# Conv and dynamic-filter layers over four images: norm statistics of all images in the first conv stage, six product buffers, every second broadcast by transfer

## The chip, the cores and the metric

The kernel runs on one core of one Trainium2 chip. The metric is the device time of one execution in microseconds (us); the median of three runs is the time of a kernel. The profile is of one further execution.

## The reference

Two layers over x of 4 images, 256 channels, 48 x 48, all in float32 (shortened):

```python
# layer 0
g = group_norm(x, 32 groups)                  # over 8 channels and all pixels
h = relu(batch_norm(conv3x3(g, conv_w) + conv_b))
q, k, v = einsum(qkv_w, h) + qkv_b            # 8 heads of 32
attn = softmax(q^T k * 32**-0.5)              # 2304 x 2304 per head
x = x + proj_w @ (v attn^T) + proj_b
# layer 1
g = group_norm(x, 32 groups)
guidance = conv3x3(g, W_cat)                  # 45 maps: 9 for each dilation
outs = [g]
for i, d in enumerate((1, 6, 12, 24, 36)):
    w = softmax(guidance[:, 9*i:9*i+9], axis=1)
    outs.append(sum over the 9 taps k of shifted(g, d, k) * w[:, k])
y = conv1x1(concat(outs), W_scale)            # 1536 -> 256 channels
x = x + batch_norm_over_all_images(y)
```

## The kernel before, in words

Channels lie on the 128 partitions in two halves (NH = 2); the 48 rows of an image go in six chunks of eight rows (NCK = 6, CH = 384 pixels). The order of instructions on each engine is written out by the program (a manual schedule): what is emitted first on an engine runs first, and waits are put in where data need them.

The main loop runs over b = 0 to 4. In step b the program emits, in one stretch, the filters of image b-1 (layer 1) merged with the conv and q, k, v of image b (layer 0), and after it the attention of image b. So the stages in time are: the conv stage of image 0 alone; attention 0; joint stretch 1 (filters of image 0, conv of image 1); attention 1; joint stretch 2; attention 2; joint stretch 3; attention 3; the last stretch (filters of image 3 alone); and the end, where y of all images is scaled and added.

**The conv stage** (`conv_qkv`, `conv`) makes a 3 x 3 convolution with transformed rows: TensorE's matmuls (line 851) go through two PSUM banks (tag "c"), ScalarE and VectorE take the results (lines 797 to 820), `relu` writes `hid`, then q, k (line 884) and v (line 905) are made. In the conv stage of image 0 VectorE also makes the transformed weights, which SP stores to memory (line 716) and later stretches read back (line 679); from image 1 on GpSimd instead of VectorE forms the transformed inputs.

**The first norms.** The conv of an image needs the group norm of its x. For image 0 it is made at the very start. For the others `stats_of` loads the image in twelve pieces of 128 x 384 through two buffers (`xst`, line 1519, on SP's queue) and takes `bn_stats` of each (line 605, VectorE). `first_norms` is a generator that makes them one step at a time; `merged` puts one step between matmuls whenever the conv's matmul time has grown by a given amount (from 40 000 ns on, each 2000 ns in the first conv stage, each 4000 ns later). In step 0 it makes images 1 and 2, in step 1 image 3. `Norm.finish` turns the sums of one image into mean and reciprocal deviation: `bn_aggr` (VectorE), a matmul with the group matrix, a copy and two squares (ScalarE), two more matmuls, then add, square root (ScalarE, with its table) and reciprocal. Image 1 is finished in step 0; images 2 and 3 are finished in the prologue of joint stretches 1 and 2, at the places called `beside` in `dynamic_filters`.

**The filters** (`dynamic_filters`). The softmaxed filter maps of a chunk are in a tile `w`, and are stored to memory too (`w_d`). Each chunk has 36 to 39 taps, 222 in a stretch. For each tap:

1. the filter map is broadcast to all partitions in a PSUM bank `wb` (three banks in joint stretches): by a TensorE matmul with a one-hot column (line 1406); or, for a third of the taps (list `sent`), by a transfer that reads `w_d` into a buffer `wbs` (three buffers, issued on ScalarE's queue, line 1351) and a ScalarE copy into PSUM (line 1403);
2. VectorE multiplies it with the shifted input (`prod`, line 1463), through five buffers (PRODS); the first tap of each dilation goes straight to `cat` (line 1437);
3. GpSimd adds the product to `cat` (line 1480). A "split" tap is divided: VectorE does one half whole (lines 1447, 1449), GpSimd adds the other (line 1452).

Finished `cat` tiles go through the 1 x 1 convolution (`mix`, line 1290), whose result is copied to y (line 1317).

**The planner.** While it emits, the program keeps a clock for PE, DVE, ACT and POOL (`Clock`), with a cost for each instruction, and decides by it: `fill` lets TensorE do conv work of the next image until the next `wb` bank is free; a tap is split when GpSimd would end over 4500 ns (SPLIT) after VectorE; and a sent broadcast goes through ScalarE only where it would be in time:

```python
late = max(clock.t["ACT"], spot + 150, there + 150) + 300
if (c, k) in number and late <= max(clock.t["DVE"], clock.t["PE"], spot + 150):
```

Here `there` is the issue plus 3000 ns and `spot` the time at which the bank is free. Otherwise the matmul is emitted, though the transfer was made. `fetch` issues transfers up to three sent broadcasts ahead, as far as the buffers reach and the chunk's filters are made.

Of the kernel before, what the change touches and what calls it, by code (L numbers as in the profile page):

```python
# [8 lines left out]
F32 = mybir.dt.float32  # L9
F32R = mybir.dt.float32r  # L10
AF = mybir.ActivationFunctionType
# [4 lines left out]
B, C, HH, WW = 4, 256, 48, 48  # L16
N = HH * WW
P = 128
NH = C // P
# [4 lines left out]
CH = R * WW  # L24
NCK = N // CH
# [9 lines left out]
SAFE = 60.0  # L35
LENT = (2, 5, 8, 11, 14)
CATS = 4
PRODS = 5
SLACK = 3000.0
SPLIT = 4500.0  # L40
BEHIND = 0.0
# [7 lines left out]
def conv_preact_kernel(  # L49
# [12 lines left out]
    nc = tc.nc  # L62

    const = ctx.enter_context(tc.tile_pool(name="const", bufs=1))
    small = ctx.enter_context(tc.tile_pool(name="small", bufs=2))
# [82 lines left out]
        nc.vector.tensor_tensor(bn_t, bn_t, vec[:, BN_B, :], ALU.add)  # L148
        return bn_s, bn_t

    def batch_norm_of(yst, pool, tag):

        ymv = pool.tile([P, NH, 2], F32, tag="ymv", name=f"ymv_{tag}")
        ysc = pool.tile([P, NH], F32, tag="ysc", name=f"ysc_{tag}")
        ysh = pool.tile([P, NH], F32, tag="ysh", name=f"ysh_{tag}")
        for o in range(NH):
            nc.vector.bn_aggr(ymv[:, o, :], yst[:, o].rearrange("p c s -> p (c s)"))
# [374 lines left out]
    with tc.tile_pool(name="w", bufs=1) as wpool, tc.tile_pool(  # L532
        name="act", bufs=1
# [37 lines left out]
        yst = wpool.tile([P, NH, B * NCK, 6], F32, tag="yst", name="yst")  # L571
# [24 lines left out]
        class Norm:  # L596


            def __init__(self, tag, b):
                self.name = f"{tag}_{b}"  # L600
                self.st = small.tile([P, NH, NCK, 6], F32, tag=f"st{tag}", name=f"st{self.name}")
                self.mv = small.tile([P, NH, 2], F32, tag=f"mv{tag}", name=f"mv{self.name}")

            def part(self, h, c, t):
                nc.vector.bn_stats(self.st[:, h, c, :], t)

            def finish(self, psum_tile):

                mean = small.tile([P, NH], F32, tag="gmean", name=f"gmean_{self.name}")
                rstd = small.tile([P, NH], F32, tag="grstd", name=f"grstd_{self.name}")  # L610
# [13 lines left out]
                yield  # L624

                pv = psum_tile(f"pv_{self.name}")
                nc.tensor.matmul(pv[:, :NH], gmat, mv[:, :, 1], start=True, stop=False)
                nc.tensor.matmul(pv[:, :NH], gmat, d2, start=False, stop=True)
                rstd_of(rstd, pv[:, :NH])
                self.mean, self.rstd = mean, rstd  # L630

            def shift_of(self):
                self.shift = small.tile([P, NH], F32, tag="gshift", name=f"gshift_{self.name}")
# [25 lines left out]
        def slot(tag, bufs):  # L659

            ends = free.setdefault(tag, [])
            return ends[-bufs] if len(ends) >= bufs else 0.0
# [439 lines left out]
            for _, _, _, y0, y1, x0, x1 in taps_of(c, n)  # L1102
        )

        def dynamic_filters(b, ao, chunk, norm, other, pools, beside):


            ps_w, ps_y, ps_m, work1 = pools
# [109 lines left out]


            alone = b == B - 1  # L1220
            ready = {}


            next(beside, None)
            while chunk < NCK:
                project(b, chunk, ao, ps_y.tile([P, 2, 512], F32, tag="y", name=f"pp_{b}_{chunk}"), norm)
                chunk += 1
            table(AF.Sqrt)
            run(2400)
            for at, _ in enumerate(norm.finish(misc)):  # L1230
                if at:
                    next(beside, None)
                run((600, 700)[at])
            for _ in beside:
                pass
            table(AF.Exp)

            for r0, r1 in ((0, 2 * R + 1), (2 * R + 1, HH)):
# [64 lines left out]
            def done(c):  # L1303
# [24 lines left out]
                else:  # L1328
                    for o in range(NH):
                        nc.sync.dma_start(out=rows_of(y_d[b, :, o, cols]), in_=rows[:, o])  # L1330

            sent = [
# [2 lines left out]
                for j, (k, _, _, y0, y1, _, _) in enumerate(  # L1337
                    t for n in range(len(DILATIONS)) for t in taps_of(c, n)
                )
                if j % 3 == 2 and (c or j > 8)  # L1340
            ]
            landed = {}
            number = {key[:2]: i for i, key in enumerate(sent)}
# [20 lines left out]
            for c in range(NCK):  # L1364
# [21 lines left out]
                for j, (n, at, (k, oy, ox, y0, y1, x0, x1)) in enumerate(taps):  # L1386
# [49 lines left out]
                    if at == 0:  # L1436
                        nc.vector.tensor_tensor(catv, wb, src, ALU.mult)
                        end = summed = clock("DVE", ns, given)
                    elif split:
                        prod = work1.tile(  # L1440
                            [P, NH, CH], F32, tag="prod", name=f"prod_{b}_{c}_{k}", bufs=PRODS
                        )
                        pv = prod[:, 0, : nr * ncol].rearrange("p (r w) -> p r w", w=ncol)
                        pw = wb[:, 0]
                        nc.vector.tensor_tensor(pv, pw, src[:, 0], ALU.mult)
                        first = clock("DVE", half, given, slot("prod", PRODS))
                        nc.vector.tensor_tensor(pw, pw, src[:, 1], ALU.mult)
                        dst = catv[:, 1, l0:l1, x0:x1]
                        nc.vector.tensor_tensor(dst, dst, pw, ALU.add)
                        end = clock("DVE", 2 * half)  # L1450
                        dst = catv[:, 0, l0:l1, x0:x1]
                        nc.gpsimd.tensor_tensor(dst, dst, pv, ALU.add)
                        summed = max(clock("POOL", added / 2 + 90, first), end)
                        free["prod"].append(clock.t["POOL"])
                    else:
                        if single:
                            mixed("single", 2 * NH)
                        tag, bufs = ("single", 3) if single else ("prod", PRODS)
# [4 lines left out]
                        nc.vector.tensor_tensor(pv, wb, src, ALU.mult)  # L1463
                        end = clock(
                            "DVE", ns, given, 0.0 if single else slot("prod", PRODS)
                        )
                    free["wb"].append(end)
                    if single:
# [29 lines left out]
            if alone:  # L1498
                for o in range(NH):
                    nc.sync.dma_start(out=x1_3[:, o], in_=x1_d[B - 1, :, o])  # L1500
                for c in range(len(y_2), NCK):
                    t = work1.tile([P, NH, CH], F32, tag="prod", name=f"yp_{c}", bufs=PRODS)
# [88 lines left out]
        for b in range(B + 1):  # L1591

            with tc.tile_pool(name=f"work1_{b}", bufs=2) as work1, tc.tile_pool(
# [11 lines left out]
                if b < B:  # L1605
# [38 lines left out]
                        u_next = weights(ORDER[0])  # L1644
                    def first_norms():

                        for i in (1, 2) if b == 0 else (b + 2,):
                            if i < B:
                                norms[i] = Norm("n0", i)
                                yield from stats_of(i, work1, norms[i])  # L1650
                            if i == 1:
                                table(AF.Sqrt)
                                yield from finished(1)
                                table(AF.Exp)

                    def finished(i):
                        yield from norms[i].finish(psc)
                        norms[i].shift_of()

                    stats = first_norms()  # L1660
                    other = merged(
                        conv_qkv(b, pads[b % 2], psc, weights, u_next, work1, between), 40000.0,
                        4000.0 if b else 2000.0, stats,
                    )
                if b == 0:
                    for j, _ in enumerate(other):
# [15 lines left out]
                else:  # L1682
                    if b == B:
# [32 lines left out]

                    dynamic_filters(
                        b - 1, ao, chunk, norm1, other, (ps_w, ps_y, ps_m, work1),
                        finished(b + 1) if b + 1 < B else iter(()),
                    )  # L1720
                    if b == B:
                        finish(work1)
# [112 lines left out]
```

## Time and profile before

| what | value |
|---|---|
| median of three runs | 2888.27 us (2886.0 to 2889.01) |
| the profiled execution | 2885.45 us |
| its span | 2883.7 us |
| busy: PE, DVE, ACT, POOL | 2721.6, 2381.2, 1671.8, 1187.6 us |
| first conv stage | 145.4 us |
| attention of images 0 to 3 | 369.5, 370.7, 373.7, 373.6 us |
| joint stretches 1 to 3 | 320.6, 313.9, 314.0 us |
| last stretch, and the end | 263.2, 39.1 us |

The stages are cut where the first score matmul of an attention starts and where its last denominator starts. PE is TensorE's matmuls and PEld its weight loads, DVE is VectorE, ACT ScalarE, POOL GpSimd and SP the sync engine, which issues transfers. A line such as "L1480 POOL ... xcount | busy, mean ns | idle before" is a group of equal instructions from one line of the kernel. A float32 matmul stands in the trace as two records.

### The profile page before, as it was taken

What the parts mean: (1) busy time and instruction counts of PE and PEld (TensorE: products, weight loads), DVE (VectorE), ACT (ScalarE), POOL (GpSimd) and SP (SyncE); (2) the same over time, 40 slices, a digit from 0 to 9 for tenths busy, and PEclk for the clock granted to TensorE, in tenths of its full rate; (3) what the DMA queues carried; (4) which work ended last, traced back from release to release, by engine and by line L of the source; (5) the groups of instructions that cost most, each with busy time, mean ns of one, the idle gap of its engine ahead of it and who ended that gap; (6) DMA issues with size and microseconds to landing.
All of it is one profiled execution on the core that took longest, in us unless ns stands there. A gap on an engine that the chain in (4) does not pass through costs nothing. (4 is left out here: it accounts for less than half of the span.)

```text
span 2883.7 us, 43644 instructions
## 1 busy us (share of the span) xinstructions
PE 2721.6 (94%) x16950; PEld 1199.6 (42%) x16950; DVE 2381.2 (83%) x2570; ACT 1671.8 (58%) x2105; POOL 1187.6 (41%) x1000
## 2 busy tenths in 40 slices
PE   7999999899999999999999999999999999989994
PEld 5722224556542222455662222355654222244562
DVE  6488888789879988878977898978986988987886
ACT  3488888322349888712238888842234888861124
POOL 1000000798840010399890001079985001006893
PEclk9999999999999999999999999999999999999997
DMA  4524445132353444323225444423223345435225
GB/s 171 126 64 100 98 99 112 48 88 85 71 105 82 103 105 110 78 65 89 54 56 116 98 95 110 100 62 88 65 56 69 75 98 113 100 80 217 57 70 207
DMA packets 148199, 272.94 MB, mean 95 GB/s; under 512 B 66760, under 2 KB 117008, under 8 KB 146192
## 3 DMA queue, kind: packets, MB, share of 16 engines
q0 software_dynamic: 23264, 128.10, 19.5%
q1 hardware_dynamic: 82384, 87.31, 10.8%
q10 hardware_dynamic: 42336, 54.66, 7.5%
q8 instruction: 135, 2.21, 0.3%
q14 instruction: 80, 0.66, 0.1%
HBM read 115.02 MB, written 32.33 MB: 51 GB/s over the span
## 5 line engine op out<-in xcount | busy, mean ns | idle before, releaser
L999 DVE TENSOR_TENSOR acc<-acc,p 128x2048 f32<-128x2048 f32 (+1 forms) x572 | 1061.2, 1855 | 116.3 <-ACT p L963 66.5
L1480 POOL TENSOR_TENSOR cat<-cat,prod 128x752 f32<-128x752 f32 (+9 forms) x661 | 883.3, 1346 | 142.0 <-DVE prod L1463 105.5
L963 ACT ACTIVATE p<-se 128x1536 f32<-128x1536 f32 x648 | 938.5, 1448 | 0.0
L954 PE MATMUL so<-q,k 32*128 32x512 f32 (+1 forms) x1440 | 731.2, 595 | 23.5 <-ACT p L962 17.1
L954 PE MATMUL se<-q,k 32*128 32x512 f32 (+1 forms) x4320 | 740.0, 595 | 0.0
L983 PE MATMUL num<-p,vT 128*32 128x512 f32 (+1 forms) x5760 | 705.4, 562 | 4.3 <-ACT p L963 2.4
L1463 DVE TENSOR_TENSOR prod<-wb,pad 128x384 f32<-128x384 f32 (+8 forms) x687 | 482.7, 737 | 92.7 <-POOL cat L1480 51.3
L962 ACT ACTIVATE p<-so 128x512 f32<-128x512 f32 x648 | 388.4, 599 | 198.1 <-PE se L954 84.7
L954 PEld LDWEIGHTS so<-q,k 32*128 32x128 f32 x1440 | 217.1, 184 | 542.6 <-ACT p L962 494.4
L1003 POOL DMA_DIRECT2D scratch<-p x124 | 105.6, 852 | 766.7 <-ACT p L963 571.1
L1290 PE MATMUL py<-cat,wsc 128*128 128x384 f32 x960 | 348.9, 493 | 9.1 <-POOL cat L1480 7.8
L1403 ACT COPY wb<-ws 128x384 f32<-128x384 f32 (+3 forms) x260 | 121.7, 468 | 365.7 <-DVE prod L1463 243.8
L983 PEld LDWEIGHTS num<-p,vT 128*32 128x32 f32 x5760 | 133.1, 108 | 479.9 <-issue 446.9
L1406 PE MATMUL wb<-w,pick 128*128 128x384 f32 (+3 forms) x628 | 299.8, 511 | 18.9 <-DVE prod L1463 10.4
L1001 POOL DMA_DIRECT2D scratch<-p x32 | 17.9, 559 | 570.7 <-ACT p L963 360.4
L954 PEld LDWEIGHTS se<-q,k 32*128 32x128 f32 x4320 | 227.7, 184 | 4.4 <-ACT p L963 4.1
L1290 PEld LDWEIGHTS py<-cat,wsc 128*128 128x128 f32 x960 | 175.8, 191 | 113.9 <-POOL cat L1480 24.3
L1406 PEld LDWEIGHTS wb<-w,pick 128*128 128x128 f32 x628 | 116.9, 191 | 130.2 <-DVE prod L1463 51.4
L851 PE MATMUL pc<-cv_q,u 128*128 128x288 f32 x576 | 159.8, 411 | 7.1 <-DVE cv_q L742 6.4
L1137 PE MATMUL pg<-pad,wcat 128*45 128x384 f32 x864 | 160.7, 504 | 4.5 <-DVE pad L592 4.5
L851 PE MATMUL pc<-cv_k,u 128*128 128x288 f32 x576 | 156.8, 410 | 4.2 <-ACT m L797 2.4
L884 PE MATMUL pq<-hid,wqkv 128*128 128x384 f32 x384 | 136.6, 494 | 11.5 <-DVE yt L786 11.2
(224 smaller groups left out, 2311.8 us busy)
## 6 DMA issues: line engine op xcount, KB each, us to landing
scratch<-p POOLq DMA_DIRECT2D x156, 768.0 KB, 5.7
ws<-w_d ACTq DMA_DIRECT2D x256, 192.0 KB, 3.2
pad<-in_x SPq DMA_DIRECT2D x14, 1152.0 KB, 14.9
u<-u_d SPq DMA_DIRECT2D x18, 768.0 KB, 4.7
x_d<-pad SPq DMA_DIRECT2D x48, 192.0 KB, 2.6
xst<-in_x SPq DMA_DIRECT2D x36, 192.0 KB, 2.3
y_d<-y SPq DMA_DIRECT2D x15, 384.0 KB, 3.4
u_d<-u SPq DMA_DIRECT2D x6, 768.0 KB, 3.7
```

Source lines behind the costliest of these rows:

```text
L851: nc.tensor.matmul(m, u[:, h, kx, o * P : (o + 1) * P], halves[g][:, h, i, :, kx : kx + WW], start=(h == 0 and kx == 0), stop=(h == NH - 1 ...
L884: nc.tensor.matmul(pq[:, :CH], wqkv[:, i, s, g * P : (g + 1) * P], hid[:, i, cols], start=(i == 0), stop=(i == NH - 1),)
L954: nc.tensor.matmul(dst[:, at : at + n], k_[r, g, m * P : (m + 1) * P], q[r, g, q0 : q0 + n], start=True, stop=True,)
L962: nc.scalar.activation(p[:, 0, :], s1, AF.Exp, scale=QS)
L963: nc.scalar.activation(p[:, 1:, :], s3, AF.Exp, scale=QS)
L983: nc.tensor.matmul(st["num"][r, at : at + n], vT[:, m, g * P + j * D : g * P + (j + 1) * D], p[:, j, at : at + n], start=(m == 0 and not s ...
L999: nc.vector.tensor_tensor(st["acc"][:, js], other[:, js], p[:, js], ALU.add)
L1137: nc.tensor.matmul(pg[64 * s : 64 * s + NG, :CH], wcat[:, ii, k, :], window(gn, ii, cc * R, k // 3 - 1, k % 3 - 1), start=(i == 0 and k == 0),
L1290: nc.tensor.matmul(to, wsc[:, n * NH + i, o * P : (o + 1) * P], rhs(i), start=(n == 0 and i == 0), stop=(last and i == NH - 1),)
L1406: nc.tensor.matmul(pw[:, : nr * WW], pick[:, k : k + 1].to_broadcast([P, P]), w[:, l0 * WW : l1 * WW], start=True, stop=True,)
L1463: nc.vector.tensor_tensor(pv, wb, src, ALU.mult)
L1480: nc.gpsimd.tensor_tensor(dst, dst, pv, ALU.add)
```

## The change

- All first norms of images 1 to 3 are made in the first conv stage: `first_norms` takes the statistics of each image and aggregates them, and then finishes all three between one pair of table loads. `merged` starts it at 20 000 ns and steps each 1500 ns. In later steps there is nothing to merge, so the two `xst` buffers are not needed there, and the `beside` places in `dynamic_filters` are gone. Each image gets its own mean, deviation and shift tiles.
- The joint stretches have six product buffers instead of five; the last stretch keeps five.
- In the joint stretches every second tap is in the list `sent` instead of every third; the last stretch keeps a third. What is in time is decided as before, and `wbs` keeps three buffers.

A new argument `ymv` of `batch_norm_of` is given by no caller.

```diff
-PRODS = 5
+PRODS = 6
...
-                self.st = small.tile([P, NH, NCK, 6], F32, tag=f"st{tag}", name=f"st{self.name}")
-                self.mv = small.tile([P, NH, 2], F32, tag=f"mv{tag}", name=f"mv{self.name}")
+                self.st = small.tile([P, NH, NCK, 6], F32, tag="st" + tag[:2], name=f"st{self.name}", bufs=1 + (tag != "n1"))
+                self.mv = small.tile([P, NH, 2], F32, tag=f"mv{tag}", name=f"mv{self.name}", bufs=1)
...
             alone = b == B - 1
+            prods = PRODS - alone
             ready = {}
...
-            next(beside, None)
             while chunk < NCK:
...
             for at, _ in enumerate(norm.finish(misc)):
-                if at:
-                    next(beside, None)
                 run((600, 700)[at])
-            for _ in beside:
-                pass
             table(AF.Exp)
...
+            share = 3 if alone else 2
...
-                if j % 3 == 2 and (c or j > 8)
+                if j % share == share - 1 and (c or j > 8)
...
-                            [P, NH, CH], F32, tag="prod", name=f"prod_{b}_{c}_{k}", bufs=PRODS
+                            [P, NH, CH], F32, tag="prod", name=f"prod_{b}_{c}_{k}", bufs=prods
...
-                        for i in (1, 2) if b == 0 else (b + 2,):
-                            if i < B:
-                                norms[i] = Norm("n0", i)
-                                yield from stats_of(i, work1, norms[i])
-                            if i == 1:
-                                table(AF.Sqrt)
-                                yield from finished(1)
-                                table(AF.Exp)
-
-                    def finished(i):
-                        yield from norms[i].finish(psc)
-                        norms[i].shift_of()
-
-                    stats = first_norms()
+                        rest = {}
+                        for i in range(1, B):
+                            norms[i] = Norm(f"n0{i}", i)
+                            yield from stats_of(i, work1, norms[i])
+                            rest[i] = norms[i].finish(psc)
+                            next(rest[i])
+                        table(AF.Sqrt)
+                        for i in range(1, B):
+                            yield from rest[i]
+                            norms[i].shift_of()
+                        table(AF.Exp)
+
+                    stats = first_norms() if b == 0 else iter(())
                     other = merged(
-                        conv_qkv(b, pads[b % 2], psc, weights, u_next, work1, between), 40000.0,
-                        4000.0 if b else 2000.0, stats,
+                        conv_qkv(b, pads[b % 2], psc, weights, u_next, work1, between), 20000.0,
+                        1500.0, stats,
                     )
...
                     dynamic_filters(
                         b - 1, ao, chunk, norm1, other, (ps_w, ps_y, ps_m, work1),
-                        finished(b + 1) if b + 1 < B else iter(()),
                     )
```

More of the change, by code (lines that the diff above doesn't have):

```diff
@@ L149, in conv_norm, with batch_norm_of @@
         return bn_s, bn_t
-    def batch_norm_of(yst, pool, tag):
-        ymv = pool.tile([P, NH, 2], F32, tag="ymv", name=f"ymv_{tag}")
+    def batch_norm_of(yst, pool, tag, ymv=None):
         ysc = pool.tile([P, NH], F32, tag="ysc", name=f"ysc_{tag}")
         ysh = pool.tile([P, NH], F32, tag="ysh", name=f"ysh_{tag}")
-        for o in range(NH):
-            nc.vector.bn_aggr(ymv[:, o, :], yst[:, o].rearrange("p c s -> p (c s)"))
+        if ymv is None:
+            ymv = pool.tile([P, NH, 2], F32, tag="ymv", name=f"ymv_{tag}")
+            for o in range(NH):
+                nc.vector.bn_aggr(ymv[:, o, :], yst[:, o].rearrange("p c s -> p (c s)"))
         rstd_of(ysc, ymv[:, :, 1])
@@ L600, in __init__ @@
                 self.name = f"{tag}_{b}"
-                self.st = small.tile([P, NH, NCK, 6], F32, tag=f"st{tag}", name=f"st{self.name}")
-                self.mv = small.tile([P, NH, 2], F32, tag=f"mv{tag}", name=f"mv{self.name}")
+                self.tag = tag
+                self.st = small.tile([P, NH, NCK, 6], F32, tag="st" + tag[:2], name=f"st{self.name}", bufs=1 + (tag != "n1"))
+                self.mv = small.tile([P, NH, 2], F32, tag=f"mv{tag}", name=f"mv{self.name}", bufs=1)
             def part(self, h, c, t):
@@ L607, in finish @@
             def finish(self, psum_tile):
-                mean = small.tile([P, NH], F32, tag="gmean", name=f"gmean_{self.name}")
-                rstd = small.tile([P, NH], F32, tag="grstd", name=f"grstd_{self.name}")
+                mean = small.tile([P, NH], F32, tag=f"gmean{self.tag}", name=f"gmean_{self.name}", bufs=1)
+                rstd = small.tile([P, NH], F32, tag=f"grstd{self.tag}", name=f"grstd_{self.name}", bufs=1)
                 d2 = small.tile([P, NH], F32, tag="gd2", name=f"gd2_{self.name}")
@@ L632, in shift_of @@
             def shift_of(self):
-                self.shift = small.tile([P, NH], F32, tag="gshift", name=f"gshift_{self.name}")
+                self.shift = small.tile([P, NH], F32, tag=f"gshift{self.tag}", name=f"gshift_{self.name}", bufs=1)
                 nc.vector.scalar_tensor_tensor(
@@ L1103, in conv_preact_kernel, with dynamic_filters @@
         )
-        def dynamic_filters(b, ao, chunk, norm, other, pools, beside):
+        def dynamic_filters(b, ao, chunk, norm, other, pools):
             ps_w, ps_y, ps_m, work1 = pools
@@ L1445, in dynamic_filters @@
                         nc.vector.tensor_tensor(pv, pw, src[:, 0], ALU.mult)
-                        first = clock("DVE", half, given, slot("prod", PRODS))
+                        first = clock("DVE", half, given, slot("prod", prods))
                         nc.vector.tensor_tensor(pw, pw, src[:, 1], ALU.mult)
@@ L1457, in dynamic_filters @@
                             mixed("single", 2 * NH)
-                        tag, bufs = ("single", 3) if single else ("prod", PRODS)
+                        tag, bufs = ("single", 3) if single else ("prod", prods)
                         prod = work1.tile(
@@ L1464, in dynamic_filters @@
                         end = clock(
-                            "DVE", ns, given, 0.0 if single else slot("prod", PRODS)
+                            "DVE", ns, given, 0.0 if single else slot("prod", prods)
                         )
@@ L1501, in dynamic_filters @@
                 for c in range(len(y_2), NCK):
-                    t = work1.tile([P, NH, CH], F32, tag="prod", name=f"yp_{c}", bufs=PRODS)
+                    t = work1.tile([P, NH, CH], F32, tag="prod", name=f"yp_{c}", bufs=prods)
                     y_2.append(t)
```

## The prediction

> **What bounds the kernel now.** The program makes its order at build time and does not leave it, so I cut the span where the scores begin and end and read the busy times of each stretch: first conv stage, attention of image 0, joint stretch 1 (filters of image 0 beside the conv stage of image 1), attention of image 1, joint stretches 2 and 3. The columns are the stretch, its length, then busy us (instructions) of PE, PEld, DVE, ACT, POOL, the granted clock, DMA share, GB/s. The attentions in between are not touched by the change and are left out.
>
> ```profile
> 0.00:145.40 145.40, 124.12 (x478) 91.85 (x478) 80.98 (x162) 56.08 (x92) 7.75 (x27) 0.99 0.51 149
> ...
> 514.90:835.50 320.60, 299.21 (x1196) 186.11 (x1189) 260.44 (x411) 82.87 (x170) 283.47 (x217) 0.98 0.27 71
> ...
> 1206.20:1520.10 313.90, 297.96 (x1192) 185.77 (x1186) 251.52 (x399) 82.76 (x170) 283.20 (x217) 0.99 0.24 65
> ...
> 1893.80:2207.80 314.00, 297.91 (x1186) 185.25 (x1179) 251.18 (x394) 82.10 (x166) 283.44 (x217) 0.98 0.23 65
> ```
>
> In a joint stretch three engines are nearly full: PE 95%, POOL 90%, DVE 80%. PE's figure flatters it: it takes conv matmuls whenever a broadcast slot is not free, and busy matmuls overlap. POOL has no taps in the first 35 us of the stretch (only conv inputs), and from 1237 to 1515 it is busy 253.6 of 278 us. The waits of joint stretch 2 (DVE, then POOL, then ACT) say who waits for whom: waiter, what it waited for, us, times, longest.
>
> ```profile
> DVE prod L1463 <- POOL cat L1480: 14.8, 20, 1.6
> DVE prod L1463 <- PE wb L1406: 6.5, 12, 1.1
> ...
> DVE cat L1437 <- PE wb L1406: 2.4, 5, 0.6
> DVE prod L1463 <- ACT wb L1403: 2.1, 2, 1.7
> ...
> POOL cat L1480 <- DVE prod L1463: 13.7, 10, 3.2
> ...
> ACT wb L1403 <- DVE prod L1463: 63.1, 31, 4.7
> ACT wb L1403 <- DMA ws<-w_d: 8.1, 3, 3.8
> ```
>
> DVE and POOL wait for each other, about 14 us each way, so they bound the stretch together. In time order the two kinds lie apart: all of DVE's waits for POOL but seven come before 1365, and from 1366 to 1420 (conv outputs, softmax) DVE is busy 50.3 of 54 us while POOL falls to 20.4 of 30 between 1400 and 1430. Broadcasts that are late cost DVE 6.5 + 2.4 + 2.1 = 11 us.
>
> **Part 1: the statistics leave joint stretch 1.** It holds twelve loads of image 3 and their statistics, and lasts 320.60 against 313.95, the mean of the two that hold none: 6.65 us more.
>
> ```profile
> L605 DVE BATCH_NORM_STATS2 stn<-xst 128x6 f32<-128x384 f32 x12 | 6.6, 548 | 0.0
> ...
> POOL cat L1480 <- DVE prod L1463: 20.2, 12, 3.2
> ```
>
> Twelve by 0.548 is 6.6 us of DVE, and POOL's waits for products rise by 20.2 - 13.7 = 6.5 us (waits of joint stretch 1). So DVE's extra work reaches the end one for one: taking it away gives **-6.65 us** (bounds 0 and -6.65). The finish of image 2's norm leaves stretch 1's prologue and that of image 3 leaves stretch 2's; stretch 2, which has one, and stretch 3, which has none, differ by 0.1 us: nothing, covered by the conv matmuls run in that prologue.
>
> **Part 2: they arrive in the first conv stage.** Twelve loads on SP's queue, twelve statistics (6.6 us), and the finishing of two more images (each about eight small DVE, four ACT and three PE instructions). There DVE is busy 81 of 145 us; from 35 us on every wait of DVE in time order is for PE, ACT or a load, and PE has no gap but 0.3 us where image 1's norm is finished. Two more such finishes: +0.6, taken as **+0.7 us**. The planner's spacing falls from 2.0 to 1.5 us for each statistic, by its clock; two of them (3.0) must hold a load (2.3 us to landing) and its 0.33 us issue. If the load is late, DVE stands with conv outputs queued behind; PE's two conv banks, 2.7 us of matmuls each (12 records, of which 22 or 23 start in 5 us), cover a wait of about 1 us. SP's wait for a free buffer has the stores of the transformed weights behind it, which are next read in joint stretch 1. Without the cover the upper bound is the 6.6 us themselves; no gain is possible, since nothing leaves this stage.
>
> **Part 3: the sixth product buffer, three joint stretches.** It lets DVE stand one more product ahead when it enters its crowded part, so POOL runs dry one addition later: the mean addition is 1.35 us (L1480, 883.3 us in 661). Once in each stretch: **-1.35 us**, -4.05 in all. In a steady POOL-bound part a deeper queue is worth nothing. The bounds: POOL's whole 13.7 us of waits, and a loss, because a POOL that is busier lengthens DVE's work on SBUF. The row (conv stage 1 with POOL idle, then joint stretch 2):
>
> ```profile
> L810 DVE TENSOR_TENSOR cs<-cs 128x288 f32<-128x288 f32 x4 | 1.8, 458 | 0.1
> ...
> L810 DVE TENSOR_TENSOR cs<-cs 128x288 f32<-128x288 f32 x4 | 7.0, 1752 | 0.1
> ```
>
> The same instruction is 3.8 times as long beside POOL's additions. The sixteen such conv outputs of a stretch take 21.2 us (8 x 0.994, 4 x 1.752, 4 x 1.542) where the first conv stage takes 7.2; if all came to the longest seen, 1.96, that would be +10.2 us. They are nearly always blocked already, so I leave it out of the sum.
> The Trainium skill speaks against this part: "SBUF — State Buffer", section "SBUF: two separate sides", says that VectorE and GpSimd share one port pair as an exclusive lock, and that a VectorE instruction with two SBUF inputs is blocked for the whole of a GpSimd instruction. The rows above agree in kind. By the rule alone each of the sixteen would be blocked for up to one addition, 16 x 1.35 = 21.6 us, against 14.0 measured; the change could then add at most 7.6 us a stretch, an estimate.
>
> **Part 4: every second broadcast instead of every third is transferred.** Counting the taps by the loop's own ranges, 106 instead of 71 of a stretch's 222 broadcasts are sent for. The planner used 63 of 71 (63 ACT copies, 159 PE broadcasts). A transfer is issued two sent broadcasts ahead, so its lead falls from six taps to four. From the times of the products in joint stretch 2, 69 of 71 have a lead over 3.5 us today; with every second sent, 99 of 106 have over 3.0, 89 over 3.5, 73 over 4.0, where the planner asks for about 3.5. Less the six that it refuses beyond that count, 83: **20 copies more** a stretch (10 to 35). Each takes 0.28 us from PE (1324.75 to 1325.03 between two starts) and gives ACT 0.469 us. PE: -5.6 us, ACT: +9.4 on 82.8, and about 20 more waits of a microsecond for a free bank, with relu, q/k and y copies queued behind them on ACT, and PE's conv banks and DVE's q/k maxima waiting for those. That is the added wait.
> What reaches the end is what DVE waits for: 17 waits of 8.9 us in 159 PE broadcasts are 0.056 each, 2.1 us in 63 copies 0.033 each. Twenty exchanged: -1.1 + 0.7 = -0.4. If PE's time came through in full: -5.6. If copies are late as in the last stretch, where the lead is three taps: DVE waited 6.1 us in 71 copies, 0.086 each, so 83 x 0.086 - 2.1 = +5.0. I take **-1.0 us**, near the DVE rows since DVE and POOL are what bounds, -3.0 in all.
>
> **Sum:** -6.65 + 0.7 - 4.05 - 3.0 = -13.0 us. The profiled execution took 2885.45 us (span 2883.7), so 2872.5; the median of three runs, 2888.27, is 2.8 above it, so 2875.3, forecast 2875.
>
> **Rivals.** *Statistics cost the same anywhere* (0.11): DVE in the first conv stage makes PE late by 6.6, and parts 3 and 4 cancel: 2888. For it: they cost one for one in stretch 1. Against: 64 us of idle DVE and a PE without gaps.
> *The copies are late* (0.17), the other side: ACT, in order, stands on transfers with half the taps' cover gone, and everything it evacuates stands behind. Price: +5.0 at the taps three times, no gain from the buffer: -6.65 + 0.7 + 15 = +9, 2897. It decides from 2.0 us of added wait a stretch on, where it eats part 1. For it: ACT waited 48.4 us, 22 times, for transfers in the last stretch; against: only 8.1, three times, in stretch 2, and the planner's refusal.
> *PE, POOL and DVE are relieved together* (0.19): PE's 5.6 us come through, and POOL loses about 3 us of waits: -6 - 3 x 8.6 = -32, 2856; half way is 2864. For: all three are above 80%, so one relief alone can show little. Against: nothing takes DVE's 251 us away.
> *Little is done* is inside the forecast: if only ten more copies pass, the result is 2877. The forecast itself, 2866 to 2882, has 0.53.
>
> **Numbers.** About 0.2% (5.8 us) is what a measurement of this kernel can tell from no change. Faster by more: 0.53 + 0.19 = 0.72; within: 0.11; slower: 0.17. The range takes most of the two outer cases: 2858 to 2893.
>
> **What would show it.** Joint stretch 1 as long as the others; the first conv stage within 2 us of 145.4; L1403 near 83 a stretch and L1406 near 139; POOL's waits for products below 13.7 us; ACT's waits for transfers below 20 us a stretch. The prediction is wrong if DVE's waits for L1403 exceed 5 us a stretch, or if the sixteen conv outputs grow beyond 21 us.

## The result

Over five runs each the changed kernel takes 2868.53 us (2866.46 to 2873.75) and the kernel before 2886.0 us (2885.14 to 2889.01): a ratio of 0.9939, 95% interval 0.9925 to 0.9954, or 13 to 22 us less. The profiled execution takes 2869.78 us, its span is 2868.0.

Cut as in the prediction, the busy times by stretch of the changed kernel (start and end, length, then busy us of PE, PEld, DVE, ACT, POOL, granted clock, DMA share, GB/s) are:

```profile
0.00:157.50 157.50, 127.89 (x491) 93.85 (x491) 88.63 (x184) 57.73 (x100) 7.74 (x27) 0.98 0.55 160
157.50:523.60 366.10, 363.26 (x3001) 102.50 (x3000) 326.74 (x213) 325.56 (x347) 30.83 (x39) 1.00 0.40 90
523.60:833.50 309.90, 290.80 (x1161) 180.16 (x1154) 251.90 (x401) 93.48 (x191) 281.72 (x217) 0.99 0.29 87
833.50:1206.60 373.10, 367.21 (x2997) 102.95 (x3000) 327.65 (x214) 325.00 (x346) 30.92 (x39) 0.99 0.48 104
1206.60:1515.90 309.30, 290.85 (x1161) 180.38 (x1154) 251.78 (x401) 93.80 (x191) 280.79 (x217) 0.99 0.32 87
1515.90:1885.80 369.90, 366.06 (x3000) 102.52 (x3000) 326.81 (x214) 325.45 (x346) 30.88 (x39) 0.99 0.48 105
1885.80:2195.50 309.70, 290.79 (x1161) 180.28 (x1154) 252.59 (x401) 93.55 (x191) 281.56 (x217) 0.99 0.30 87
2195.50:2564.30 368.80, 365.88 (x2998) 102.56 (x3000) 326.84 (x214) 318.33 (x334) 30.91 (x39) 0.99 0.44 97
```

The first conv stage is longer by 12.1 us. The joint stretches are shorter by about 10, 4 and 4 us. And the attentions, which the change does not touch, are shorter by 10.6 us in sum. The table cuts every kernel exactly where the first score matmul of an attention and its last denominator start (the windows above are up to 0.4 us off these cuts):

| kernel | first conv stage | joint stretches 1, 2, 3 | their sum | attentions, sum | profiled execution's span |
|---|---|---|---|---|---|
| before | 145.4 | 320.6, 313.9, 314.0 | 948.5 | 1487.5 | 2883.7 |
| before, again | 144.8 | 320.9, 314.2, 312.8 | 947.9 | 1487.7 | 2883.3 |
| changed | 157.5 | 310.2, 309.6, 310.1 | 929.9 | 1476.9 | 2868.0 |
| changed, again | 159.2 | 310.7, 309.5, 310.2 | 930.4 | 1478.3 | 2869.5 |
| norms only | 159.1 | 313.0, 314.4, 314.0 | 941.4 | 1487.8 | 2890.2 |
| norms, buffer | 159.5 | 309.5, 308.4, 309.0 | 926.9 | 1486.8 | 2874.8 |
| norms, half | 158.8 | 317.0, 314.3, 315.1 | 946.4 | 1475.9 | 2883.5 |
| changed, from 40 000 ns | 147.9 | 310.5, 309.2, 309.9 | 929.6 | 1477.7 | 2856.4 |
| the same, a third sent | 148.7 | 309.7, 308.9, 308.7 | 927.3 | 1483.2 | 2863.3 |

So the difference of the two spans, -15.7, is +12.1 (conv) - 18.6 (joint) - 10.6 (attentions) + 1.4 (last stretch and end).

Where the first conv stage lost its time is seen in DVE's order of time in the changed kernel (start, us, line, and in brackets the idle time before and what ended it):

```profile
49.51 1.74 DVE L712 TENSOR_TENSOR u<-u,wc 128x1536 f32<-128x1536 f32 x1
51.17 0.55 DVE L608 BATCH_NORM_STATS2 stn<-xst 128x6 f32<-128x384 f32 x1
55.85 1.04 DVE L608 BATCH_NORM_STATS2 stn<-xst 128x6 f32<-128x384 f32 x2 [4.13 <-DMA xst<-in_x]
58.85 0.56 DVE L608 BATCH_NORM_STATS2 stn<-xst 128x6 f32<-128x384 f32 x1 [1.96 <-DMA xst<-in_x]
...
65.37 1.01 DVE L608 BATCH_NORM_STATS2 stn<-xst 128x6 f32<-128x384 f32 x2
68.35 1.12 DVE L608 BATCH_NORM_STATS2 stn<-xst 128x6 f32<-128x384 f32 x2 [1.97 <-DMA xst<-in_x]
71.75 0.56 DVE L608 BATCH_NORM_STATS2 stn<-xst 128x6 f32<-128x384 f32 x1 [2.27 <-DMA xst<-in_x]
72.23 0.44 DVE L807 TENSOR_TENSOR cs<-pc,m 128x288 f32<-128x288 f32 x1
72.59 0.45 DVE L808 TENSOR_TENSOR cs<-m,pc 128x288 f32<-128x288 f32 x1
```

DVE stands 4.1 us on a load at 51.7, then 2.0 more; forms the inputs from 59.3 to 65.4, so that its buffers are emptied late; and stands on two more loads. SP's order of time tells why the loads are late:

```profile
41.72 5.77 SPq L1519 DMA_DIRECT2D xst<-in_x  x3
51.28 0.33 SPq L719 DMA_DIRECT2D u_d<-u  x1
51.70 15.05 SPq L1519 DMA_DIRECT2D xst<-in_x  x7
66.84 0.38 SPq L719 DMA_DIRECT2D u_d<-u  x1
68.94 10.57 SPq L1519 DMA_DIRECT2D xst<-in_x  x7
```

After three loads SP stands on the store of weights that DVE finishes only at 51.25 (its line 712 above); the next load goes out at 51.7, behind those 768 KB, and lands 4.1 us later; DVE is already waiting for it. The other three loads that DVE waits for show another reason. With two buffers a load can go out only when DVE has done the statistic two pieces before: these three leave at 56.44, 65.95 and 68.94, each 0.03 us after such a statistic ends, and land 2.4, 2.4 and 2.8 us later, while DVE's stream holds only one more statistic of 0.55 us. In the kernel before, five of the six stores were issued before the first of these loads:

```profile
17.61 45.82 SPq L716 DMA_DIRECT2D u_d<-u  x5
63.48 8.23 SPq L1519 DMA_DIRECT2D xst<-in_x  x4
```

Only at 72.2 does DVE of the changed kernel come to the conv outputs. PE works without a gap until 65.7, has then filled both banks, and waits for DVE (PE's order of time, then waiter, what it waited for, us, times, longest):

```profile
59.68 5.98 PE L854 MATMUL pc<-cv_q,u 128*128 128x288 f32 x24
73.08 7.10 PE L854 MATMUL pc<-cv_k,u 128*128 128x288 f32 x22 [7.43 <-DVE cs L808]
```

```profile
PE pc L854 <- DVE cs L808: 7.4, 1, 7.4
```

Windows of 5 us show PE's busy time (first figure after the length) and the granted clock (third from the end):

```profile
65.00:70.00 5.00, 0.66 (x3) 0.19 (x1) 2.50 (x5) 0.00 (x0) 0.00 (x0) 0.93 0.63 226
70.00:75.00 5.00, 1.92 (x4) 1.49 (x5) 3.09 (x9) 0.00 (x0) 0.00 (x0) 0.50 0.52 144
75.00:80.00 5.00, 5.00 (x19) 3.74 (x19) 2.59 (x6) 0.00 (x0) 0.00 (x0) 0.89 0.37 101
```

PE idles 7.4 us, and then runs at half the clock before it is back. The Trainium skill, "TensorE: Matmul & The Clock Gate", "Part 1: The HAM clock gate (the "warmup" mystery)", says that an idle window of about 3.4 us lowers the clock to half until such a window has been busy; the 0.50 in the row agrees.

In joint stretch 2 the waits (DVE, POOL, ACT) answer to those shown of before:

```profile
DVE prod L1463 <- PE wb L1406: 11.9, 20, 1.6
DVE prod L1463 <- POOL cat L1480: 3.5, 6, 0.9
DVE prod L1463 <- ACT wb L1403: 3.4, 6, 1.1
...
POOL cat L1480 <- DVE prod L1463: 8.6, 9, 1.7
...
ACT wb L1403 <- DVE prod L1463: 55.6, 35, 8.4
...
ACT wb L1403 <- DMA ws<-w_d: 12.5, 8, 2.7
```

DVE's waits for POOL fell from 14.8 to 3.5 us and POOL's for DVE from 13.7 to 8.6; but DVE's waits for broadcasts by matmul rose from 6.5 to 11.9, though there are fewer of these.

### The profile page after: what moved, and what is told of

Read it like the earlier page. It is cut to its first block, busy times and chain, and to the rows that moved or that the text cites. A ratio compares the mean times of both kernels' runs of the same rounds, so it can differ in the third digit from the quotient of the medians.

```text
span 2868.0 us, 43872 instructions
## 1 busy us (share of the span) xinstructions
PE 2701.6 (94%) x16875; PEld 1185.0 (41%) x16875; DVE 2381.9 (83%) x2594; ACT 1707.3 (60%) x2180; POOL 1181.9 (41%) x1000
## 5 line engine op out<-in xcount | busy, mean ns | idle before, releaser
L1480 POOL TENSOR_TENSOR cat<-cat,prod 128x752 f32<-128x752 f32 (+9 forms) x649 | 868.7, 1348 | 130.1 <-DVE prod L1463 84.1
L1463 DVE TENSOR_TENSOR prod<-wb,pad 128x752 f32<-128x752 f32 (+9 forms) x675 | 474.6, 738 | 81.7 <-PE wb L1406 40.9
L1403 ACT COPY wb<-ws 128x384 f32<-128x384 f32 (+3 forms) x335 | 156.7, 468 | 407.2 <-DVE prod L1463 223.9
L1406 PE MATMUL wb<-w,pick 128*128 128x384 f32 (+3 forms) x553 | 269.1, 516 | 20.9 <-DVE prod L1463 13.6
L1406 PEld LDWEIGHTS wb<-w,pick 128*128 128x128 f32 x553 | 103.4, 190 | 120.3 <-DVE prod L1463 38.5
```

The lines of the kernel that those rows point to most:

```text
L1403: nc.scalar.copy(pw[:, : nr * WW], of[:, : nr * WW])
L1406: nc.tensor.matmul(pw[:, : nr * WW], pick[:, k : k + 1].to_broadcast([P, P]), w[:, l0 * WW : l1 * WW], start=True, stop=True,)
```

## The experiments

The median ratio to the kernel before stands with each run that was timed.

### Each part by itself

**Norms only**: five buffers, a third sent.

```diff
-            prods = PRODS - alone
+            prods = PRODS - 1
-            share = 3 if alone else 2
+            share = 3
```

> Only the norms are moved; five product buffers and every third broadcast sent in all stretches. My theory (each part has its own worth): first conv stage 157 us as in the changed kernel, joint stretch 1 falls from 320.6 to about 314, stretches 2 and 3 stay at 314, so about +12 - 6.6 = +5 us against before plus whatever the attentions do. Rival A (the attentions' 9.6 us come from the moved norms, not from chance): attentions 2 and 3 fall from 373.7 to about 369 here too, total about -4. Rival B (prediction's step: the statistics are hidden in the first conv stage): first conv stage 146 us, total -6.

Measured: 2890.93 us, ratio 1.0028 (1.0019 to 1.0037). The first conv stage takes 159.1, joint stretch 1 313.0, the others 314.4 and 314.0, the attentions 1487.8 in sum. So by itself the move costs: it gives 7.6 us in joint stretch 1 and loses 13.7 in the first conv stage. Rivals A and B both fall.

**Norms and the sixth buffer**: only `share = 3`.

> The norms moved and the sixth product buffer, every third broadcast sent. My theory (buffer worth one addition of 1.35 us a stretch, the rest of the 4.6 us that each stretch lost comes from the broadcasts): joint stretches near 312.6, DVE's waits for POOL near 13 us. Rival (the buffer is what counts, DVE's waits for POOL fell from 14.8 to 3.5 because of it): joint stretches near 310.5, DVE's waits for POOL below 6 us, splits 22 to 24.

Measured: 2872.68 us, ratio 0.9964 (0.9951 to 0.9978). The rival is nearer: DVE's waits for POOL are under its 6 us, and the stretches and the splits lie beyond its figures. The buffer alone takes the joint stretches from 941.4 to 926.9, 4.8 us each. Joint stretch 2 of this kernel: the stretch, and the split taps' additions on POOL alone (us, count):

```profile
1208.40:1516.80 308.40, 292.14 (x1188) 183.76 (x1182) 252.56 (x406) 81.66 (x165) 280.10 (x217) 1.00 0.25 66
...
1208.40:1516.80 308.40, 20.92 (x26) 1.00 0.25 66
```

And its waits there:

```profile
DVE prod L1463 <- PE wb L1406: 9.4, 14, 1.5
...
DVE prod L1463 <- POOL cat L1480: 5.8, 9, 1.0
...
POOL cat L1480 <- DVE prod L1463: 11.2, 11, 1.9
```

There are 26 split taps where with the norms only, and before, there are 20. By the code, VectorE waits for a product buffer later in the planner's clock when there are six, so GpSimd's lag behind it reaches the 4500 ns more often, and a tap is split. Whole and split additions take POOL 224.1 + 20.9 = 245.0 us instead of 231.7 + 16.1 = 247.8 with the norms only, and its waits fall from 13.7 to 11.2 us: together 5.3 of the 6.0 us by which this stretch is shorter (314.4 to 308.4). That accounts for the time in the trace; a run with the old splits and six buffers was not made, so the two shares are read and not tested.

**Norms and half the broadcasts**: only `prods = PRODS - 1`.

> The norms moved and every second broadcast sent, five product buffers. My theory: joint stretches near 311, about 85 copies and 135 matmul broadcasts a stretch, DVE's waits for POOL unchanged near 14 us. Rival (the buffer is what counts, and copies alone make ACT late): joint stretches 314 to 316, DVE's waits for the copies over 5 us.

Measured: 2888.44 us, ratio 1.0024 (1.0015 to 1.0034), which can't be told from the norms alone. 88 copies and 134 matmul broadcasts a stretch. The joint stretches take 946.4 instead of 941.4: my theory (311 each) falls, and the stretches lie about where the rival put them. DVE's waits for the copies are 6.2, 4.6 and 4.9 us in the three, about the 5 that it set. But DVE's waits for broadcasts by matmul rose more, though there are fewer of these. Joint stretch 2 with the norms only, and with the halved list:

```profile
DVE prod L1463 <- PE wb L1406: 5.7, 11, 1.1
```

```profile
DVE prod L1463 <- PE wb L1406: 11.5, 17, 1.6
```

DVE's waits for POOL fell there from 14.8 to 8.8 us, where my theory had them unchanged. With six buffers the cost of the halved list is 929.9 - 926.9 = 3.0 us. But the attentions of this kernel take 1475.9 instead of 1487.8.

### The first conv stage

**The statistics from 40 000 ns on.**

```diff
-                        conv_qkv(b, pads[b % 2], psc, weights, u_next, work1, between), 20000.0,
+                        conv_qkv(b, pads[b % 2], psc, weights, u_next, work1, between), 40000.0,
```

> The changed kernel with the first statistics put in from 40 000 ns of conv time on instead of 20 000, as before the change, still every 1500 ns. My theory (the 12 us of the first conv stage come from statistics whose transfers stand behind the weights' store on SP's queue while VectorE forms the inputs and weights, before 66 us): first conv stage 146 to 149 us, VectorE's waits for the transfers fall from 16.3 to under 8 us, total 8 to 11 us less than the changed kernel, about 2859. Rival (36 statistics at this pace cost the same wherever they begin): first conv stage 154 to 158, total 2868.

Measured: 2859.32 us, ratio 0.9924 (0.9908 to 0.9939); first conv stage 147.9. DVE's waits for the loads are still 9.9 us, more than I had said, but none is over 1.3 us and PE waits for none of them:

```profile
DVE stn L608 <- DMA xst<-in_x: 9.9, 17, 1.3
```

The window from 38 to 80 us, in the changed kernel and then in this one:

```profile
38.00:80.00 42.00, 34.36 (x135) 25.98 (x134) 24.65 (x45) 6.73 (x10) 0.00 (x0) 0.92 0.43 132
```

```profile
38.00:80.00 42.00, 41.79 (x173) 32.29 (x172) 24.32 (x45) 8.71 (x14) 0.00 (x0) 1.00 0.35 118
```

Between 38 and 80 us PE is busy 41.8 of 42 us; in the changed kernel it is 34.4. So 36 statistics at this pace fit the stage at 2.5 us more than 24 did; 9.6 of the 12.1 us were for the place where they began.

**The loads on GpSimd's queue**, from 20 000 ns on.

```diff
         def load(i):
-                nc.sync.dma_start(
+                nc.gpsimd.dma_start(
```

> The changed kernel with the pieces of images 1 to 3 loaded from GpSimd's queue, which has nothing else to do in the first conv stage, instead of SP's; they still begin at 20 000 ns. My theory (the loads stand on SP's queue behind the stores of the weights, so VectorE stands on them and the conv outputs behind it): the first conv stage falls from 157.5 to 147 to 150 us, VectorE's waits for the loads from 16.3 to under 6 us, total about 2860. Rival (two buffers and the pace of 1.5 us are too tight on any queue, or the statistics themselves crowd VectorE): first conv stage 154 to 158.

Measured: 2891.6 us, ratio 1.0030 (1.0021 to 1.0040); first conv stage 180.9, worse than either theory. What the loads had held back on SP's queue ran ahead (SP's order of time):

```profile
64.86 24.10 SPq L1727 DMA_DIRECT2D pad<-in_x  x4
```

These are the four loads of 1152 KB for the padded images; in the changed kernel they stand behind the small loads until 111 us. Now 4.6 MB are under way from 65 us on, with a DMA share of 0.96 or more in every 5 us until 95, and the small loads beside them make DVE wait 43.4 us in 23 waits, 6.2 the longest. The run tells nothing for or against the first theory, since it put another cause in its place.

**Four buffers and loads three ahead**, on SP's queue, from 20 000 ns on.

```diff
-            ahead = load(0)
+            ahead = [load(i) for i in range(3)]
...
-                if i + 1 < NH * NCK:
-                    ahead = load(i + 1)
+                if i + 3 < NH * NCK:
+                    ahead.append(load(i + 3))
```

> The changed kernel, statistics from 20 000 ns on, with four buffers for the pieces of images 1 to 3 and the loads issued three ahead instead of one, on SP's queue. Theory A (VectorE stands on loads that come late, and the conv outputs behind it): the first conv stage falls from 157.5 to 147 to 150 us, VectorE's waits for the loads from 16.3 to under 5. Theory B (the statistics themselves, put in before 66 us beside the inputs and the weights that VectorE makes, crowd it): 153 to 158 with few waits for the loads, and TensorE still waits 5 us or more for the conv outputs.

Measured: 2863.51 us, ratio 0.9931 (0.9915 to 0.9948); first conv stage 151.1, just outside A's numbers and further from B's:

```profile
DVE stn L608 <- DMA xst<-in_x: 5.8, 3, 3.4
...
PE pc L854 <- DVE cs L808: 1.3, 1, 1.3
```

With the statistics at the same places and only the loads earlier, 6.4 of the 12.1 us are gone, and PE's 7.4 us wait is 1.3. So late loads are the greater part of the loss. What is left against the later start (151.1 against 147.9) is not taken apart: one wait of 3.4 us for a load behind the store is still in it.

### The attentions

**The changed kernel and the kernel before, once more.**

> The changed kernel once more, unaltered, for a second profile. Theory A (the attentions' lengths belong to the kernel's arrangement): attentions 2 and 3 at 368 to 370 again, ScalarE's waits for the accumulating transfers 1 to 3 us. Theory B (they differ by chance from run to run): either may be 372 or more. Joint stretches 309 to 310.5, first conv stage 157 to 159 by both.

> The kernel before, unaltered, for a second profile. Theory A: attentions 2 and 3 at 373 to 375 again, ScalarE's waits for the accumulating transfers 8 to 9 us in each. Theory B: either may be 370 or less. Joint stretches 320, 314, 314, first conv stage 145 to 146 by both.

Measured: 2871.23 and 2885.07 us, one run each. Attentions 2 and 3 take 368.6 and 367.8 in the changed kernel (first profile 369.6, 368.4) and 374.9 and 372.9 in the one before (373.7, 373.6). Attention 0 of the changed kernel, 366.1 and 369.6, shows what chance does. So the shorter attentions 2 and 3 come back with the kernel. ScalarE's waits in attention 2 for the transfers that sum three probability tiles go with it. Before:

```profile
ACT p L962 <- DMA scratch<-p: 8.9, 9, 1.8
```

Changed:

```profile
ACT p L965 <- DMA scratch<-p: 2.9, 4, 1.1
```

With the norms and the buffer they are 8.3 us in 9 waits, with the norms and the halved list 3.1 in 5.

**A third sent, from 40 000 ns on**: `share = 3` with the start at 40 000.

> The first statistics from 40 000 ns on, six product buffers, every third broadcast sent: only the broadcasts differ from the run that began at 40 000 ns with every second. Theory A (the halved broadcasts cost the joint stretches 1 us each, but make attentions 2 and 3 about 4.5 us shorter each, for a reason that is open): joint stretches near 309, attentions 2 and 3 at 373 to 374, total 5 to 8 us above that run. Theory B (the attentions differ by chance from run to run): attentions anywhere from 368 to 374, total 2 to 3 us below that run.

Measured: 2862.81 us, ratio 0.9922 (0.9909 to 0.9936), against 0.9924 with every second sent: the timed runs don't tell the two apart. In the profiles the joint stretches are 2.3 us shorter, as in theory A, and attentions 2 and 3 are 375.1 and 371.4 against 369.1 and 369.3: attention 2 as in theory A, attention 3 less so.

**Idle transfers**: the norms alone, with some 35 transfers more in each joint stretch that nothing reads.

```diff
+                    if not alone and j % 6 == 1 and (c or j > 8):
+                        spare_t = work1.tile([P, CH], F32, tag="wbx", name=f"wx_{b}_{c}_{k}", bufs=1)
+                        nc.scalar.dma_start(
+                            out=spare_t[:, : (l1 - l0) * WW],
+                            in_=w_d[b, c, k, l0 * WW : l1 * WW].partition_broadcast(P),
+                        )
```

> The kernel with only the norms moved (five buffers, every third sent), with some 35 broadcasts more transferred in each joint stretch into a buffer that nothing reads: the traffic and the issues of the halved list without its copies and without a change of the planner's order. Theory A1 (the extra transfers themselves, by their count on the queue, shift the accumulating transfers of attentions 2 and 3): both attentions 368 to 370, ScalarE's waits for the accumulating transfers under 4 us each. Theory A2 (the order or the number of the other instructions does it): 373 to 376 as without them, waits 8 to 10 us.

Measured: 2889.48 us (one run); attentions 2 and 3 374.5 and 373.2, ScalarE's waits 6.0 and 6.8 us. The transfers alone don't make the attentions shorter: A1 falls. The lengths are those of A2; the waits lie between the two theories. They don't lengthen the joint stretches either (942.6 against 941.4).

**Every second broadcast in joint stretch 1 alone.**

```diff
-            share = 3 if alone else 2
+            share = 2 if b == 0 else 3
```

> The changed kernel with every second broadcast sent in joint stretch 1 alone, every third in 2 and 3. Theory A1 (transfers counted up over the run): attentions 2 and 3 in between, or other than both 369 and 374. Theory A2 (the stretch just before an attention sets it): attentions 2 and 3 at 373 to 375 as where a third is sent, attention 1 at 371 to 373. Joint stretch 1 310, 2 and 3 308.5 to 309, by either.

Measured: 2870.07 us (one run); attentions 2 and 3 369.1 and 373.0, attention 1 370.9, joint stretches 310.0, 308.1, 308.5. Attention 2 is short after a joint stretch with a third sent, so A2 falls too; nor is the outcome what A1 named. And here length and wait come apart: ScalarE waits 6.1 us for the accumulating transfers in the short attention 2 and 4.7 us in the long attention 3.

**Four steps lent instead of five**, from 40 000 ns on.

```diff
-LENT = (2, 5, 8, 11, 14)
+LENT = (2, 6, 10, 14)
```

> The kernel with statistics from 40 000 ns on, and in the attentions four steps (2, 6, 10, 14) instead of five whose three probability tiles are summed by accumulating transfers, four steps apart instead of three. Theory (the attentions' spread is ScalarE waiting for a probability tile that a late transfer still reads): ScalarE's waits for these transfers fall under 1 us in each attention and all four last 365 to 368 us, total 2850 to 2855. Rival (VectorE, which sums 1.6 us more in each unit, becomes the bound): attentions 370 or more, total above 2860.

Measured: 2857.7 us, ratio 0.9907 (0.9891 to 0.9924). The attentions take 367.3, 369.6, 370.4 and 369.3, 1476.6 in sum against 1477.7, and ScalarE still waits 3 to 5 us in each for the transfers. The theory's condition (waits gone) didn't come about and its lengths didn't either, nor did the rival's; whether it is better than with five can't be told from the two ratios.

The kernel with the later start has a shorter span than the changed kernel has in either profile (2856.4 against 2868.0 and 2869.5); its ratio's interval still overlaps that of the changed kernel. Sixth buffer, norms and a start at 40 000 ns carry it; sending every second broadcast is not needed for it, since its ratio with a third sent is the same.

## Why the prediction was right or wrong

The total was forecast at 2875, -13.0 us; measured are 2868.5 and -17.5. (The forecast starts from 2888.27, the median of three runs; that of five is 2886.0.) It is inside the range and on the forecast side, but that is in part luck: by the profiles the first conv stage came out 11.4 us above its term, the joint stretches 4.9 us below theirs, and the attentions, which are not in the sum, 10.6 us shorter.

- **Part 1, the statistics out of joint stretch 1: right.** Forecast -6.65, measured -7.6 with the norms alone (320.6 to 313.0). The finishes that left stretches 1 and 2 were worth nothing, as said: stretch 2 is 314.4 without one.
- **Part 2, the first conv stage: the step failed.** Forecast +0.7 with an upper bound of 6.6, measured +12.1, and +14.1 with the norms and the buffer. The step that failed is that a load is in time because two steps of 1.5 us hold its 2.3 us to landing and its issue of 0.33. It priced the closer pace, and not that the statistics now begin 20 000 ns earlier; I had not asked what stands on SP's queue in front of the loads there. One load came 4.1 us late, behind a store. Two buffers turn round in 3.0 us (55.85 to 58.85 for two statistics), no faster than the pace asks, so the lateness was not made up, and three more loads were 2.0 to 2.3 us late. DVE, in order, came to the conv outputs so late that PE stood 7.4 us with both banks full. The cover of about 1 us for these banks was not the error: the lateness was a multiple of it. The bound was wrong in kind: work that is added to an idle engine costs its own time at most, but a wait that is added costs the wait, and then PE's clock. With the old start 9.6 of the 12.1 us are gone.
- **Part 3, the sixth buffer: right in sign, too small.** Forecast -1.35 a stretch, measured -4.8. The step took the plan as fixed. The planner reads the buffer count, and with six it split 26 taps instead of 20 (24 with the halved list), so that POOL lost work (2.8 us in joint stretch 2), and its waits fell by 2.5 us, not by one addition of 1.35. The loss by longer conv outputs did not come: the sixteen take 19.9 us in joint stretch 2 of the changed kernel (4 x 1.789 + 8 x 0.852 + 4 x 1.475) instead of 21.2, so the room for 7.6 us that the Trainium skill's lock left was not used.
- **Part 4, half the broadcasts: the count right, the value wrong in sign.** Forecast 83 copies and 139 matmul broadcasts, measured 88 and 134. In joint stretch 2 DVE's waits for copies stayed under the 5 us that I had set (3.4), and ACT's for transfers under 20 (12.5). But the joint stretches became longer by 1.0 us each with six buffers and by 1.7 with five, not shorter by 1.0. The price of 0.056 us for each matmul broadcast assumed that waits fall with their number. Counted as there (products and first taps, joint stretch 2), they rose: with five buffers from 8.1 us for 159 to 13.3 for 134, with six from 11.8 for 160 to 14.3 for 134. So about half of the changed kernel's rise over before (8.9) came with the buffer. PE is busy 7 us less in stretch 2 than before (290.9 against 298.0), but it is already at 292.1 with the norms and the buffer, so little of this is the list's.
- **What was missing: the attentions.** I left them out as untouched. They gave 10.6 us, of which 9.3 lie in attentions 2 and 3, and in the profiles this is the whole gain of part 4. The timed runs hardly show that gain. Halving the list shortens the profiled spans by 6.7 us (norms only), 6.8 (norms and buffer) and 6.9 (from 40 000 ns), about 0.0023; the timed ratios go from 1.0028 to 1.0024, from 0.9964 to 0.9939 and from 0.9922 to 0.9924. Three of these six profiles are of an extreme run: the slowest of five in two kernels that send a third, the fastest of ten in one that sends half.
- **Rivals.** *Statistics cost the same anywhere* named the right stage and less than the measured price. *The copies are late* did not occur. *Relieved together* half did: POOL lost work and waits, but PE's saved time did not come through, and beyond part 1 the joint stretches gave 11.5 us (941.4 to 929.9) of its 26.

What stays open is why attentions 2 and 3 become shorter with the halved list. Shown is that they do so in every kernel that sends every second broadcast in all joint stretches and lends five steps (six profiles, 367.5 to 370.4 us, where six that send a third have 371.4 to 375.9), and that ScalarE waits less for the accumulating transfers in them (1.2 to 4.3 us against 6.0 to 10.0). Against the added transfers and against the stretch just before as the cause speaks one run each. That these waits set the length is not shown: with every second broadcast in joint stretch 1 alone the attention with the longer waits is the shorter one. Attention 1 lies between 368.4 and 374.7 us over the same profiles, and there the two lists overlap.

## What to carry to other kernels

An instruction that depends on a transfer and is put into an in-order engine's stream is not free because the engine has idle time: price the wait that it may hold, and what stands behind it, and place it after the large transfers of the same queue (9.6 us here), or issue its loads further ahead (6.4 us). Where a program plans its own order, a buffer count is also an input of the plan: ask which decisions read it, since here the planner's answer took about as much off GpSimd's work (2.8 us in a stretch) as came off its waits (2.5 us). And taking loads off one queue lets the transfers behind them go: the large ones then meet the small ones.

## What the runs showed of the hardware

Two things were unexpected. Small loads of 192 KB that land in 2.3 us (median) in the kernel before made VectorE wait up to 6.2 us each when four loads of 1152 KB were under way, though they were issued from another queue. And two stretches with the same instructions, attentions 2 and 3, differ by 4 to 6 us between the kernel before and the changed one, in both profiles of each. In most kernels the shorter ones go with shorter waits of ScalarE for transfers that are issued in the stretch itself, but not in all; the cause is open.
